# Mixing two tanh terms: one accumulator with av and minus av, in place of a difference on GpSimd

## The chip, the cores and the metric

The kernel runs on one core of one Trainium2 chip. A core has five engines that run side by side: TensorE (PE in the profile; its weight loads are listed as PEld), VectorE (DVE), ScalarE (ACT), GpSimd (POOL) and SyncE (SP), which here only issues DMA transfers. Each engine takes its own instructions in order; semaphores tie the engines to one another. The metric is the device time of one execution in microseconds (us). Lower is better.

## The reference

Four graph layers work on x of shape (8, 2048, 64): 8 batches, 2048 nodes, 64 features. Each layer takes a layer norm and a ReLU of x, computes its own output from that, and adds the output to x. The change lies at the end of the first layer. There every node has two vectors of 64 features: `industry`, a product with the adjacency matrix, and `g`, an attention over hyperedges. They are mixed with a softmax over two scores:

```
def attn_scores(f):
    return jnp.tanh(f @ fcW + fcb) @ av
pair = jnp.stack([industry, g], axis=2)
coefs2 = jax.nn.softmax(attn_scores(pair), axis=-1)
out = jnp.einsum('bnk,bnkf->bnf', coefs2, pair)
```

`fcW` maps 64 features to 128, and `av` has 128 entries. A softmax over two scores needs only their difference d: the weight of `industry` is (1 + tanh(d / 2)) / 2. The second layer begins with the norm of the mixed x, and then with the product of the adjacency matrix with it.

## The kernel before, in words

Features lie on the partitions and nodes along the free axis. Two batches share the 128 partitions (64 each), so there are four batch pairs q. The 2048 nodes are cut into four chunks of 512. `mix` (L619) goes over chunks and, within a chunk, over the four q: 16 pairs of chunk and q in all. The two inputs are `ind` (industry) and `g`, whole in SBUF.

`attend` (L644) does the first half of a pair. For `ind` and then for `g`, two matmuls with `fcw` fill a PSUM tile p1 of 128 x 2 x 512 (one half for each batch of the pair), and ScalarE writes its tanh into a slot of `ring` (L653); the ring has four slots, two for each of two pairs in flight. GpSimd subtracts the two tanh (L655) into dt, one of two buffers. At q = 0 the chunk's x is loaded by SP (L658), and GpSimd adds g to x for this q (L660). The loop in `mix` calls `attend` for the next pair before it finishes the present one: two matmuls multiply dt with `av`, copied into 64 equal columns, into the two 64-partition halves of a PSUM tile pd; ScalarE takes tanh of half of it (L684); VectorE forms ind - g (L686), scales it by the result (L687) and adds it to x (L688). So every partition of a batch holds the same score difference.

After the four pairs of a chunk, x is stored to DRAM (L241) and the norm for the next layer begins (`norm_parts`, L253): matmuls with `center` take off the mean, ScalarE squares (L264) and takes the ReLU (L269), matmuls with `to_rows` gather the means of the squares, ScalarE takes the root (L272, behind a load of its table), VectorE the reciprocal (L273). The generator then stops and is taken up after one of the next chunk's pairs: matmuls with `from_rows` spread the reciprocal back over the partitions, and VectorE writes the product (L634), two instructions for each q. The PSUM tiles of center, to_rows, from_rows and of the transposes come from one pool of three banks, `bank`.

`each` (L760), called ahead of a chunk's first pair, brings the rows of g for this chunk by four indirect DMAs on GpSimd (L763), transposes them on PE (L769), four transposes to a tile, and copies them into `g` by ScalarE and VectorE in turn (L172, L174).

The next layer (`chebyshev_layer`) begins with `by_node`, which turns the normed x into rows by transposes (L1312), split into a rounded high part by ScalarE (L232) and a rest by VectorE (L233). `adj_product` (L302) loads the adjacency in pieces (SP, L313) into three buffers, casts each on ScalarE (L325), and multiplies both parts on PE. All matmuls issued through the helper `mm` carry its line, L166, in the profile; they are told apart by the names of their tiles.

The order of the instructions on each engine isn't the order of the Python lines: the tile framework that the kernel is built with orders them, and an instruction whose buffers are free early can be placed ahead of other work. The order of the built program is therefore looked at beside the diff. The code has a second path for inputs that don't pass a check of their structure; it calls `mix` too, and does not run here.

Of the kernel before, what the change touches and what calls it, by code (L numbers as in the profile page):

```python
# [7 lines left out]
F = mybir.dt.float32  # L8
# [11 lines left out]
P = 128  # L20
NB = 8
N = 2048
D = 64
# [3 lines left out]
CW = 512  # L27
# [100 lines left out]
class Kernel:  # L128
# [490 lines left out]
    def mix(self, slots, ind, g, fcw, av, each=None):  # L619


        nc, tc = self.nc, self.tc
        big = [slots.tile([P, 2, NP, CW], F, name=f"mix{i}", tag=f"q{6 + i}") for i in range(3)]
        ring = slots.tile([P, 4, 2, CW], F, name="tanh", tag="q9")

        end = [slots.tile([P, 2, NP, CW], F, name=f"end{i}", tag=f"q{4 + i}") for i in range(2)]
        end = end[0][:, 0], end[0][:, 1], end[1][:, 0]
        xe, xo = self.chebyshev(slots)

        def write(q, ch, xr, scale):  # L630
            s = slice(ch * CW, (ch + 1) * CW)
            for i, dst in enumerate((xe, xo)):
                h = slice(i * D, (i + 1) * D)
                nc.vector.tensor_mul(dst(q)[h, s], xr[h], scale[h])  # L634


        with (
            tc.tile_pool(reuse_waits="tile", name="mix", bufs=2) as w,
            tc.tile_pool(reuse_waits="tile", name="mix_ps", bufs=1, space=PSUM) as ps,
        ):  # L640
            def bank():
                return ps.tile([P, CW], F, name="bank", bufs=3)

            def attend(ch, q):  # L644

                s = slice(ch * CW, (ch + 1) * CW)
                th = [ring[:, 2 * (q % 2) + i] for i in range(2)]
                for i, src in enumerate((ind, g)):
                    p1 = ps.tile([P, 2, CW], F, name="p1", bufs=2)
                    for half in range(2):  # L650
                        h = slice(half * D, (half + 1) * D)
                        self.mm(p1[:, half], fcw[h], src(q)[h, s])
                    nc.scalar.activation(th[i], p1, AF.Tanh, bias=self.col("fcb"))  # L653
                dt = w.tile([P, 2, CW], F, name="dt")
                nc.gpsimd.tensor_sub(dt, th[0], th[1])  # L655
                if q == 0:
                    bufs[ch] = end if ch == NC - 1 else [b[:, ch % 2] for b in big]
                    nc.sync.dma_start(bufs[ch][0], self.xs[0][ch])  # L658
                x = bufs[ch][0]
                nc.gpsimd.tensor_add(x[:, q], x[:, q], g(q)[:, s])  # L660
                return dt

            norm = iter(())
            bufs = {}
            if each is not None:
                each(0, bank)
            pairs = [(ch, q) for ch in range(NC) for q in range(NP)]
            ahead = attend(*pairs[0])
            for ch in range(NC):
                s = slice(ch * CW, (ch + 1) * CW)  # L670
                x, sq, xr = bufs[ch]
                for q in range(NP):
                    dt = ahead
                    if q == NP - 1 and each is not None and ch + 1 < NC:
                        each(ch + 1, bank)
                    if (ch, q) != pairs[-1]:

                        ahead = attend(*pairs[NP * ch + q + 1])
                    pd = ps.tile([P, CW], F, name="pd")
                    for half in range(2):  # L680
                        self.mm(pd[half * D : (half + 1) * D], av[:, :D], dt[:, half])

                    t2 = w.tile([P, CW], F, name="t2")
                    nc.scalar.activation(t2, pd, AF.Tanh, scale=0.5)  # L684
                    df = w.tile([P, CW], F, name="df")
                    nc.vector.tensor_sub(df, ind(q)[:, s], g(q)[:, s])  # L686
                    nc.vector.scalar_tensor_tensor(df, t2, 1.0, df, op0=OP.add, op1=OP.mult)  # L687
                    nc.vector.scalar_tensor_tensor(  # L688
                        x[:, q], df, 0.5, x[:, q], op0=OP.mult, op1=OP.add
                    )  # L690
                    if q < 2:
                        next(norm, None)
                self.store_x(0, ch, x)
                std = w.tile([P, CW], F, name="std")
                norm = self.norm_parts(ch, x, xr, sq, std, bank, write, nc.scalar)
            for _ in norm:
                pass
# [1666 lines left out]
```

## Time and profile before

| what | value |
|---|---|
| median of 3 runs | 2153.69 us (2149.0 to 2154.99) |
| profiled execution, its own time | 2148.51 us |
| its span, first to last instruction | 2146.8 us |
| mean granted TensorE clock | 0.932 |
| busy share PE / DVE / ACT / POOL | 89 / 53 / 33 / 33% |
| GpSimd differences (L655) | 16, 40.6 us busy |

The profile is one execution. It has a page with busy shares, 40 equal slices of the span, the chain of work that ended last and the costliest groups of instructions; the trace behind it also answers questions about a stretch: busy time of each engine, waits (who waited for whom), groups of instructions with their mean length, and the timeline. In a group, the numbers after the bar are its busy time in us, its mean length in ns, and the idle time of the engine just before it with what ended it. A float32 matmul of 512 columns shows as two records, so the two matmuls of a pd are four. The granted clock is the share of full speed at which TensorE was let run.

### The profile page before, as it was taken

To read this page: it belongs to the slowest core of one execution; us is meant where nothing else is said; L and a number is where in the kernel's file an instruction comes from. 1 tells how busy PE (TensorE), PEld (TensorE's weight loads), DVE (VectorE), ACT (ScalarE), POOL (GpSimd) and SP (SyncE) were. 2 spreads that over 40 slices of the span, in tenths; PEclk is the share of its full clock that TensorE was granted. 3 is DMA by queue.
4 is the path that set the end of the run, shared out by engine and by line. 5 is a ranking of instruction groups with operands and counts; after the bars stand their busy time and mean duration, and the time that the engine had idled before them with its cause. 6 is when DMAs were issued, how large, how long until landed. Compare 5 with 4: busy or idle time off the path is not lost. (4 is left out here: it accounts for less than half of the span.)

```text
span 2146.8 us, 21291 instructions
## 1 busy us (share of the span) xinstructions
PE 1914.5 (89%) x7461; PEld 1153.1 (54%) x7466; DVE 1134.1 (53%) x1932; ACT 714.7 (33%) x1351; POOL 702.4 (33%) x595
## 2 busy tenths in 40 slices
PE   5868999977779999999999998999999999679875
PEld 1425766642237774353443543677777666345432
DVE  7877677737660224424334255698603222249774
ACT  6412555535543440020100201335335333258400
POOL 0000466765300006617357065001000000177770
PEclk8868999988869999999999999999999999879997
DMA  8230333441034360140320401456533443475665
GB/s 320 82 110 4 102 104 118 133 171 43 36 94 134 119 177 14 32 125 0 102 56 5 118 1 60 138 186 235 166 118 125 151 145 131 158 210 162 180 181 180
DMA packets 108797, 253.66 MB, mean 118 GB/s; under 512 B 20912, under 2 KB 21056, under 8 KB 101376
## 3 DMA queue, kind: packets, MB, share of 16 engines
q1 hardware_dynamic: 89264, 181.45, 26.7%
q0 software_dynamic: 17104, 66.47, 10.0%
q10 hardware_dynamic: 2304, 4.20, 0.5%
q8 instruction: 63, 1.03, 0.2%
q14 instruction: 62, 0.51, 0.1%
HBM read 218.30 MB, written 33.78 MB: 117 GB/s over the span
## 5 line engine op out<-in xcount | busy, mean ns | idle before, releaser
L325 ACT CAST adj<-adj_t 128x512 fp32r<-128x512 f32 x384 | 237.3, 619 | 685.9 <-PE pp L166 349.5
L1421 POOL TENSOR_TENSOR acc<-acc,y 128x512 f32<-128x512 f32 x224 | 277.1, 1268 | 444.9 <-DVE y L1416 444.9
L166 PE MATMUL pp<-adj,hi 128*128 128x512 f32 x1280 | 364.4, 404 | 4.4 <-ACT adj L325 4.2
L166 PE MATMUL pk<-q,w 128*128 128x512 f32 (+1 forms) x1024 | 356.5, 609 | 1.8 <-ACT q L1389 1.6
L166 PE MATMUL pp<-adj,lo 128*128 128x512 f32 x1280 | 356.3, 398 | 0.0
L166 PEld LDWEIGHTS pp<-adj,hi 128*128 128x128 f32 x1280 | 241.2, 190 | 77.0 <-issue 16.2
L166 PEld LDWEIGHTS pp<-adj,lo 128*128 128x128 f32 x1280 | 242.7, 190 | 55.6
L166 PEld LDWEIGHTS pk<-q,w 128*128 128x128 f32 (+1 forms) x1024 | 136.2, 188 | 210.2 <-issue 165.9
L1416 DVE SCALAR_TENSOR_TENSOR y<-pk,bias,q 128x512 f32<-128x512 f32 x224 | 157.7, 745 | 142.7 <-PE pk L166 133.2
L166 PE MATMUL acc<-q,ident 128*128 128x512 f32 x416 | 203.4, 615 | 28.4 <-DVE q L2151 16.4
L2061 POOL DMA_INDIRECT ring<-f_rows,near x121 | 140.3, 1160 | 67.5 <-issue 30.2
L166 PEld LDWEIGHTS acc<-q,ident 128*128 128x128 f32 x416 | 76.7, 195 | 104.7 <-issue 47.7
L2165 POOL IOTA q<- 128x2048 int32 x1 | 1.8, 1834 | 316.6 <-PE p L166 316.6
L166 PE MATMUL pp<-adj,x_ind_hi 128*128 128x512 f32 x256 | 94.7, 487 | 2.1 <-DVE q L751 1.9
L166 PE MATMUL bank<-std,from_rows 32*128 32x512 f32 x128 | 45.5, 858 | 54.4 <-DVE std L273 34.5
L1853 POOL TENSOR_TENSOR q<-q,beta 128x512 f32<-128x512 f32 x57 | 67.9, 1192 | 54.6 <-DVE beta L1829 30.8
L1416 DVE SCALAR_TENSOR_TENSOR acc<-pk,bias,q 128x512 f32<-128x512 f32 x32 | 22.6, 746 | 118.1 <-PE pk L166 118.1
L2132 DVE TENSOR_TENSOR q<-ring,e 128x1024 f32<-128x1024 f32 x58 | 70.0, 1218 | 9.3 <-PE acc L166 9.1
L273 DVE RECIPROCAL std<-std 128x512 f32<-128x512 f32 x16 | 53.6, 3351 | 36.7 <-ACT std L272 36.6
L166 PE MATMUL pp<-adj,x_ind_lo 128*128 128x512 f32 x256 | 71.7, 399 | 0.0
L1543 POOL DMA_INDIRECT q<-in_adj_dram,order x15 | 17.2, 1146 | 160.3 <-DVE top L1557 134.0
L166 PEld LDWEIGHTS pp<-adj,x_ind_hi 128*128 128x128 f32 x256 | 48.5, 190 | 38.7 <-issue 23.7
(410 smaller groups left out, 2695.8 us busy)
## 6 DMA issues: line engine op xcount, KB each, us to landing
adj_t<-in_adjT_dram SPq DMA_DIRECT2D x128, 512.0 KB, 3.9
adj_t<-in_adjT_dram SPq DMA_DIRECT2D x128, 256.0 KB, 3.3
rows<-in_adj_dram SPq DMA_DIRECT2D x16, 1024.0 KB, 6.0
q<-x SPq DMA_DIRECT2D x10, 1024.0 KB, 4.8
x<-q SPq DMA_DIRECT2D x9, 1024.0 KB, 4.0
q<-in_embT_dram SPq DMA_DIRECT2D x8, 1024.0 KB, 12.1
x_ch<-in_xT_dram SPq DMA_DIRECT2D x4, 1024.0 KB, 6.0
h_rows<-q SPq DMA_DIRECT2D x16, 256.0 KB, 3.6
```

The costliest lines, as they stand in the source:

```text
L166: self.nc.tensor.matmul(out, lhsT, rhs, start=start, stop=stop)
L273: nc.vector.reciprocal(std, std)
L325: nc.scalar.copy(moving, at[:, i])
L1416: nc.vector.scalar_tensor_tensor(y, pks[b, half], bias[:, b : b + 1], emb[:, b], op0=OP.add, op1=OP.mult,)
L1421: nc.gpsimd.tensor_add(acc, acc, y)
L1543: nc.gpsimd.indirect_dma_start(row, None, self.a["adj"], bass.IndirectOffsetOnAxis(ap=order[:, 1, t : t + 1], axis=0),)
L1853: self.nc.gpsimd.tensor_tensor(x, x, by.unsqueeze(2).to_broadcast([P, NB, D]), op=OP.mult)
L2061: self.nc.gpsimd.indirect_dma_start(to, None, self.kern.f_rows[:], bass.IndirectOffsetOnAxis(ap=index, axis=0))
L2132: nc.vector.tensor_tensor(y.rearrange("n i (b f) -> n i b f", b=NB), block[:, i : i + 2, : NB * D].rearrange("n i (b f) -> n i b f", b=NB) ...
L2165: nc.gpsimd.iota(whole, pattern=[[1, N]], base=0, channel_multiplier=0)
```

## The change

The tanh of both inputs go to the second product as they are. Per pair there are four matmuls instead of two: av times the first tanh opens the accumulation in each half of pd, and minus av (`less`, made once by VectorE) times the second tanh closes it. The difference on GpSimd and its two buffers are gone.

```diff
@@ -651,15 +651,16 @@
                         h = slice(half * D, (half + 1) * D)
                         self.mm(p1[:, half], fcw[h], src(q)[h, s])
                     nc.scalar.activation(th[i], p1, AF.Tanh, bias=self.col("fcb"))
-                dt = w.tile([P, 2, CW], F, name="dt")
-                nc.gpsimd.tensor_sub(dt, th[0], th[1])
                 if q == 0:
                     bufs[ch] = end if ch == NC - 1 else [b[:, ch % 2] for b in big]
                     nc.sync.dma_start(bufs[ch][0], self.xs[0][ch])
                 x = bufs[ch][0]
                 nc.gpsimd.tensor_add(x[:, q], x[:, q], g(q)[:, s])
-                return dt
-
+                return th
+
+            less = w.tile([P, D], F, name="less", bufs=1)
+            nc.vector.tensor_scalar_mul(less, av[:, :D], -1.0)
+            avs = av[:, :D], less
             norm = iter(())
             bufs = {}
             if each is not None:
@@ -670,15 +671,19 @@
                 s = slice(ch * CW, (ch + 1) * CW)
                 x, sq, xr = bufs[ch]
                 for q in range(NP):
-                    dt = ahead
+                    th = ahead
                     if q == NP - 1 and each is not None and ch + 1 < NC:
                         each(ch + 1, bank)
                     if (ch, q) != pairs[-1]:
 
                         ahead = attend(*pairs[NP * ch + q + 1])
                     pd = ps.tile([P, CW], F, name="pd")
-                    for half in range(2):
-                        self.mm(pd[half * D : (half + 1) * D], av[:, :D], dt[:, half])
+                    for i in range(2):
+                        for half in range(2):
+                            self.mm(
+                                pd[half * D : (half + 1) * D], avs[i], th[i][:, half],
+                                start=i == 0, stop=i == 1,
+                            )
 
                     t2 = w.tile([P, CW], F, name="t2")
                     nc.scalar.activation(t2, pd, AF.Tanh, scale=0.5)
```

In the built program two more things differ, both on engines that the diff doesn't name. The first four adjacency loads of the second layer (L313) stand on SP's queue directly behind the load of the last chunk's x, and three of their casts (L325) stand on ScalarE among the first pairs of the mixing; before, these loads followed the mixing's last store. And the first 16 matmuls of the second layer's adjacency product are placed between the transposes L1312, from the fifth group of four on; before, they followed them.

## The prediction

> **What bounds the kernel now.** I first read the page's slices. TensorE (PE) is busy in nine tenths of nearly every slice; the soft place is around slices 9 to 12, where its granted clock is 0.7 to 0.9. The chain that ended last covers only the last 17 us of the span, so it says nothing here. The edited code runs from 462 to 606 us ("the mixing stage"), which I split where the gather transposes of each 512-node chunk begin. Columns: stretch, its length, busy time of PE, of weight loads, of VectorE, ScalarE, GpSimd, then granted clock, DMA share, GB/s.
>
> ```profile
> 487.40:524.30 36.90, 28.53 (x91) 9.19 (x89) 28.09 (x27) 19.61 (x27) 16.16 (x9) 0.85 0.16 57
> 524.30:564.07 39.77, 30.76 (x91) 10.67 (x89) 25.65 (x25) 19.60 (x27) 16.04 (x9) 0.80 0.06 27
> 564.07:601.87 37.80, 28.47 (x91) 9.34 (x89) 26.34 (x25) 19.52 (x27) 15.96 (x9) 0.86 0.07 28
> ```
>
> Three periods, 114.5 us; no engine is full, so a chain of waits bounds them, with PE the fullest. PE idles 26.7 us of it. A mean clock near 0.84 means, if it only alternates between half and full, about 31% of the time at half. Next the waits and groups of 465 to 612 us:
>
> ```profile
> PE pd L166 <- POOL dt L655: 17.3, 5, 5.6
> PE bank L166 <- DVE q L634: 12.1, 3, 4.0
> L655 POOL TENSOR_TENSOR dt<-tanh 128x1024 f32<-128x1024 f32 x16 | 40.6, 2543 | 61.5 <-ACT tanh L653 61.4
> L686 DVE TENSOR_TENSOR df<-q,q 128x512 f32<-128x512 f32 x16 | 26.9, 1684 | 0.4
> L687 DVE SCALAR_TENSOR_TENSOR df<-t,df 128x512 f32<-128x512 f32 x16 | 26.0, 1624 | 25.0 <-ACT t L684 25.0
> L166 PE MATMUL pd<-dt,av 128*64 128x512 f32 x64 | 22.0, 773 | 17.3 <-POOL dt L655 17.3
> ```
>
> PE, which takes its work in order, stands 17.3 us in five waits for GpSimd's difference. L686 and L687 average 1.6 us, while their shortest is 0.68. Last the timeline, for the period from 564.07 and the step after the stage (start, length, engine, line, idle before):
>
> ```profile
> 570.52 1.99 PE L166 MATMUL p<-q,fcw 64*128 64x512 f32 x8
> ...
> 573.96 5.54 POOL L655 TENSOR_TENSOR dt<-tanh 128x1024 f32<-128x1024 f32 x2
> ...
> 576.79 1.08 PE L166 MATMUL pd<-dt,av 128*64 128x512 f32 x4 [4.29 <-POOL dt L655]
> ...
> 577.80 5.39 PE L166 MATMUL bank<-mix,center 128*128 128x512 f32 x8
> ...
> 591.29 2.52 DVE L687 SCALAR_TENSOR_TENSOR df<-t,df 128x512 f32<-128x512 f32 x1 [0.96 <-ACT t L684]
> ...
> 596.05 2.04 PE L166 MATMUL bank<-std,from_rows 32*128 32x512 f32 x2 [4.04 <-DVE q L634]
> ...
> 600.03 1.90 PE L166 MATMUL pd<-dt,av 128*64 128x512 f32 x4
> ...
> 623.07 10.38 PE L1312 MATMUL pt<-ident,q 64*128 64x64 f32 x100 [1.77 <-DVE lo L233]
> ...
> 637.59 2.08 PE L166 MATMUL pp<-adj,hi 128*128 128x512 f32 x4
> ```
>
> Both tanh of the pair were ready by 570.9, but GpSimd did its four adds of the chunk (568.16 to 574.0) first; the difference came at 576.8. PE sat 4.29 us, and the centers behind ran partly at half speed (0.86 us instead of 0.43 per output). At 591.29 the next difference stretched L687 to 2.52 us, which held the first L634, which frees the PSUM bank of the fourth from_rows: a second idle of 4.04 us, again followed by half speed (pd 1.90 against 1.08).
>
> **What the skill says.** "TensorE: Matmul & The Clock Gate", What's actually happening: the array clock falls to half after about one idle window of 3.4 us, and returns after about as much sustained work. The trace agrees: after the 2.20 us idle at 500.7 pd took 1.08; after 4.29 and 5.65 us it, or the centers behind it, ran at half. "GPSIMD Engine Reference", Specifications: GpSimd shares its SBUF interfaces with VectorE and contends with VectorE instructions with two SBUF inputs. L686 and L687 have two; 1.6 us against 0.68 agrees. "TensorEngine Tiling (Array Packing)", Column Tiling and Key Properties: 64-wide stationaries run as two column tiles, and changing the tiling mode drains TensorE. The two 64-row halves of pd indeed start together (two records at 500.73, two at 501.21).
>
> **The change, part by part.** *Removed:* 16 GpSimd subtractions, 40.6 us of GpSimd, so five PE waits (17.3 us) and their share of the VectorE stretching. GpSimd keeps its 16 adds, which still stretch some L686 to L688.
>
> *Added:* per pair of chunk and batch pair, four more matmul records on PE. No row accumulates onto an av product; the nearest is p, where four further records lengthen 1.13 us to 1.99: 0.86 us, or 1.62 at half clock (1.98 to 3.60 at 479). Sixteen make 13.8 us at full clock, 16.4 at clock 0.84, 26 at half. The other bound is 3.2 each at half clock, should the two halves not overlap. I take 0.86. The tanh buffers are now freed by pd, which stands on PE ahead of the p whose tanh reuses them: no new wait. The one negation on VectorE is 128x64 (a 128x1024 one, L1294, takes 0.68 us) and falls while PE waits for gathers near 457: nothing.
>
> *Moved*, by the order of the built program: without dt's two buffers, the first four loads of layer 1's adjacency (512 KB each) go on SP's queue behind the last chunk's input load (465.76 us), ahead of the chunk 0 store, and three casts (L325, 0.62 us) go on ScalarE ahead of the first t2 and the third pair's tanh. The input load takes 7.1 us to land (472.9); 512 KB at the burst's 410 GB/s is 1.3 us, so the casts can begin at 474 to 476. The fourth load waits for the second cast; behind it on SP is a store not ready before 500. In layer 1's first step, 16 adjacency matmuls are put between the transposes L1312. GpSimd's last four gathers now follow one another; used only from 560.
>
> *First chunk.* pd of pair 0 no longer waits for gathers and adds (5.65 us idle): it runs at 471.4 to 473.3, p(2) to 475.2, pd(1) to 477.1; tanh(2) behind the casts starts at 477.6, p(3) runs 478.7 to 480.6, pd(2) ends at 482.5 where the transposes began at 487.4. **-5** (-2 to -6).
>
> *One period*, walked from 564.07 at full clock (the 16 pairs are numbered 0 to 15; this is chunk 3, pairs 12 to 15): transposes and p of the first pair, with their wait for the bank, to 568.9; pd(11), now 1.87 long, to 570.8; p(13) to 572.7; pd(12) directly to 574.6; centers (4 x 0.86) to 578.1; to_rows and p(14) to 582.5; pd(13) to 584.4. ScalarE: squares until 579.6, table load 1.28, root at 581.6. VectorE: reciprocal 3.35, to 585.0. PE: three from_rows to 586.3. L687 is 0.69 now and L688 0.69, so L634's first two end at 588.6 (PE idle 2.3 us, under the window, clock stays); fourth from_rows and p(15) to 590.5; pd(14) to 592.4, where it ended at 601.9. That is -9.5, three times -28.5.
>
> The same by terms: 17.3 of waits, three times 1.83 of stretched L687 (5.5), half-clock excess about 13.7 in the periods (27 busy us at half, halved) and 2.5 in the first chunk, against 13.8 added: -25. Between -33.5 (walk, first chunk included) and -25 I take **-29**; neither counts all hops between engines.
>
> *Layer 1's first step.* Transposes and the first 16 adjacency matmuls now take 620.12 to 643.71, 23.6 us, at clock 0.5 until 642. Where the program already mixes them (670.5 to 672.6, full clock), one transpose group plus one matmul takes 0.70 against 0.23 and 0.20 apart: a switch costs about 0.27. At full clock 16 x 0.70 + 16 x 0.20 = 14.4, so VectorE's 16.5 bounds: -7. At half clock, 28: +5. I take **-2**.
>
> After that the order is as before, PE is busy 99% of 640 to 720 us, and a shift passes to the end. Sum: -29 - 2 = -31. The profiled execution took 2148.51 (span 2146.8), the median is 2153.69; 2148.5 - 31 = 2117.5, and against the median **2123**.
>
> **Rivals.** *B, the clock doesn't recover*: 17.3 + 5.5 back, 16.4 added, nothing in layer 1: -6, **2147**. For it: the clock is 0.84 even where PE is busy 75%; against: each half-speed stretch I looked at follows an idle of 4 us or the low-density transposes. *C, the interleaving of layer 1 fails* at half clock: -29 + 5 = -24, **2130**. For it: clock 0.50 all through 620 to 640. *D, slower*: the two halves of the second product don't overlap, or drain, and the clock stays low: 16 x 3.2 = 51 against 22.8, +28, **2182**; it decides once a pair's addition exceeds 22.8 / 16 = 1.4 us without clock recovery. Against: pd's four records already overlap. *That the change doesn't do what it says* can't be: no subtraction is left on GpSimd.
>
> **Numbers.** Main case 0.68 (own range 2104 to 2136), C 0.10, B 0.15, D 0.07. About 0.3% (6.5 us) is what a measurement tells from no change; B lies on that edge, so half of it counts as same. Faster 0.85, same 0.08, slower 0.07. Range 2103 to 2145: left out are D, half of B and a sliver of the main case.
>
> **What would show it.** No L655 row; pd about 1.9 us per group of eight records; PE waiting under 5 us for tanh at pd; periods near 29 us with clock above 0.95; L687 near 0.7 us; mixing ending some 29 us earlier; matmuls of L166 among L1312's. Wrong if the periods stay over 35 us, if pd's eight records take 3 us or more at full clock, or if ScalarE's casts wait past 480.

## The result, and the profile after

| | before | after |
|---|---|---|
| median, runs beside one another | 2152.06 us (2149.0 to 2154.99) | 2132.72 us (2121.22 to 2136.89) |
| ratio, with its 95% interval | | 0.9906 (0.9881 to 0.9931) |
| profiled execution, its span | 2148.51, 2146.8 us | 2136.79, 2134.9 us |
| mean granted clock of the span | 0.932 | 0.932 |

The changed kernel is 19 us faster where 31 were forecast; 2132.72 us is 10 us above the forecast median.

To find where the difference lies, both spans are cut at the same events of the trace: the first transpose of gathered rows, the first transpose of the second layer (`pt`), and the first matmul into the tile `pk`, which follows that layer's first adjacency product.

| stage (us) | before | after | difference |
|---|---|---|---|
| up to the first gather transpose | 455.9 | 458.0 | +2.1 |
| mixing | 164.2 | 140.3 | -23.9 |
| second layer, first step | 186.6 | 190.0 | +3.4 |
| all that follows | 1340.1 | 1346.6 | +6.5 |
| span | 2146.8 | 2134.9 | -11.9 |

The line numbers shift a little: L684, L686 and L687 are now L689, L691 and L692, and L1312 is L1317. L166, L325, L634 and L653 are the same. In the experiments they shift by a few lines again; the operation and the tiles in a line tell what it is. First the mixing by chunks, cut as in the prediction (stretch, length, busy time of PE, weight loads, VectorE, ScalarE, GpSimd, then granted clock, DMA share, GB/s):

```profile
484.79:515.90 31.11, 29.00 (x106) 9.70 (x104) 20.07 (x25) 19.53 (x27) 5.85 (x4) 0.95 0.18 68
515.90:547.02 31.12, 29.01 (x107) 9.80 (x105) 20.16 (x25) 19.52 (x27) 5.85 (x4) 0.95 0.08 34
547.02:579.45 32.43, 30.32 (x106) 9.90 (x104) 20.15 (x25) 19.52 (x27) 6.06 (x5) 0.90 0.08 33
```

The periods fell from 36.9, 39.8 and 37.8 us to 31.1, 31.1 and 32.4, and PE idles about 2.1 us in each, where it idled 26.7 us in the three together. The clock rose from 0.80 to 0.86 to between 0.90 and 0.95, so it isn't full. The waits and the groups of 465 to 605 us:

```profile
PE bank L166 <- DVE q L634: 7.9, 4, 2.1
```

```profile
L166 PE MATMUL pd<-tanh,av 128*64 128x512 f32 x64 | 19.8, 700 | 1.6 <-ACT t L689 1.6
L691 DVE TENSOR_TENSOR df<-q,q 128x512 f32<-128x512 f32 x16 | 18.7, 1172 | 0.4
L166 PE MATMUL pd<-tanh,less 128*64 128x512 f32 x64 | 17.6, 630 | 0.0
...
L692 DVE SCALAR_TENSOR_TENSOR df<-t,df 128x512 f32<-128x512 f32 x16 | 11.3, 703 | 24.4 <-ACT t L689 24.4
```

The five waits for GpSimd are gone, and the scaling of the difference (L692) is back at 0.70 us from 1.62. The subtraction of the inputs (L691) still averages 1.17 us: twelve of its sixteen instances take 0.68 or 0.69 us, and the four that run beside the adds that GpSimd kept take 1.51 to 5.91. What is left on PE within the periods is one wait for VectorE's L634 in each, 2.1 us at most. The timeline of the chunk from 547.02 shows what that wait does (start, length, engine, line, idle before):

```profile
555.81 1.08 PE L166 MATMUL pd<-tanh,av 128*64 128x512 f32 x4
...
556.72 1.03 PE L166 MATMUL pd<-tanh,less 128*64 128x512 f32 x4
...
557.68 3.70 PE L166 MATMUL bank<-mix,center 128*128 128x512 f32 x8
...
572.54 1.37 PE L166 MATMUL bank<-std,from_rows 32*128 32x512 f32 x2 [2.11 <-DVE q L634]
...
575.84 1.97 PE L166 MATMUL pd<-tanh,av 128*64 128x512 f32 x4
...
577.60 1.92 PE L166 MATMUL pd<-tanh,less 128*64 128x512 f32 x4
```

The second product costs what was estimated: eight records of pd from 555.81 to 557.68, 1.87 us, and the eight centers behind them run at full speed. But the fourth from_rows waits 2.11 us, and what follows it runs at half speed: 1.97 and 1.92 us for four records of pd that take 1.08 and 1.03 at full clock.

In the second layer's first step, transposes and adjacency matmuls now alternate:

```profile
601.96 0.79 PE L166 MATMUL pp<-adj,hi 128*128 128x512 f32 x1
...
602.69 0.70 PE L1317 MATMUL pt<-ident,q 64*128 64x64 f32 x8
```

All 32 groups of transposes and the first 32 adjacency matmuls took 27.3 us before (620.12 to 647.38) and take 29.9 us now (598.32 to 628.25). The mean clock over the first 40 us of this step is 0.72 before and 0.67 after; the half speed in which the step begins lasts 22.6 us before and 26.1 us after.

### The profile page after: what moved, and what is told of

Its sections match the earlier page's. It is cut to its first block, busy times and chain, and to the rows that moved or that the text cites. A ratio compares the mean times of both kernels' runs of the same rounds, so it can differ in the third digit from the quotient of the medians.

```text
span 2134.9 us, 21390 instructions
## 1 busy us (share of the span) xinstructions
PE 1929.4 (90%) x7525; PEld 1154.3 (54%) x7530; DVE 1111.8 (52%) x1933; ACT 714.7 (33%) x1351; POOL 666.9 (31%) x579
## 3 DMA queue, kind: packets, MB, share of 16 engines
q0 software_dynamic: 17104, 66.47, 10.2%
q8 instruction: 63, 1.03, 0.2%
## 5 line engine op out<-in xcount | busy, mean ns | idle before, releaser
L325 ACT CAST adj<-adj_t 128x512 fp32r<-128x512 f32 x384 | 237.3, 619 | 689.4 <-PE pp L166 345.8
L166 PE MATMUL pp<-adj,hi 128*128 128x512 f32 x1280 | 368.8, 406 | 4.9 <-ACT adj L325 3.7
L166 PE MATMUL pk<-q,w 128*128 128x512 f32 (+1 forms) x1024 | 358.3, 611 | 3.8 <-ACT q L1394 3.6
L166 PE MATMUL pp<-adj,lo 128*128 128x512 f32 x1280 | 361.1, 400 | 0.0
L166 PEld LDWEIGHTS pp<-adj,hi 128*128 128x128 f32 x1280 | 241.7, 191 | 78.4 <-issue 16.7
L166 PEld LDWEIGHTS pp<-adj,lo 128*128 128x128 f32 x1280 | 243.0, 190 | 56.4
L166 PEld LDWEIGHTS pk<-q,w 128*128 128x128 f32 (+1 forms) x1024 | 136.6, 188 | 213.5 <-issue 166.4
L166 PE MATMUL acc<-q,ident 128*128 128x512 f32 x416 | 202.7, 613 | 28.2 <-DVE q L2156 17.9
L166 PEld LDWEIGHTS acc<-q,ident 128*128 128x128 f32 x416 | 76.1, 193 | 103.8 <-issue 46.6
L166 PE MATMUL pp<-adj,x_ind_hi 128*128 128x512 f32 x256 | 94.6, 486 | 2.2 <-DVE q L756 1.9
L166 PE MATMUL bank<-std,from_rows 32*128 32x512 f32 x128 | 43.7, 858 | 48.6 <-DVE std L273 34.5
L1421 DVE SCALAR_TENSOR_TENSOR acc<-pk,bias,q 128x512 f32<-128x512 f32 x32 | 22.6, 746 | 121.5 <-PE pk L166 121.5
L166 PE MATMUL pp<-adj,x_ind_lo 128*128 128x512 f32 x256 | 71.6, 398 | 0.0
L166 PEld LDWEIGHTS pp<-adj,x_ind_hi 128*128 128x128 f32 x256 | 48.5, 189 | 38.8 <-issue 23.8
L1548 POOL DMA_INDIRECT q<-in_adj_dram,order x15 | 17.2, 1148 | 166.3 <-DVE top L1562 137.5
## 6 DMA issues: line engine op xcount, KB each, us to landing
q<-in_embT_dram SPq DMA_DIRECT2D x8, 1024.0 KB, 12.6
```

Of the source, the lines that this page charges most:

```text
L166: self.nc.tensor.matmul(out, lhsT, rhs, start=start, stop=stop)
L325: nc.scalar.copy(moving, at[:, i])
L1421: nc.vector.scalar_tensor_tensor(y, pks[b, half], bias[:, b : b + 1], emb[:, b], op0=OP.add, op1=OP.mult,)
L1548: nc.gpsimd.indirect_dma_start(row, None, self.a["adj"], bass.IndirectOffsetOnAxis(ap=order[:, 1, t : t + 1], axis=0),)
```

## The experiments

Every trace was cut into the stages above; the table collects their lengths, in us. "Kept" means that the second layer's loads, casts and first adjacency matmuls stand where they stood before the change, "moved" that they stand where the change put them. The medians come from several series; each run was timed beside the kernel before, and its ratio below refers to that.

| run | order of layer 2 | mixing | first step | what follows | median |
|---|---|---|---|---|---|
| before | kept | 164.2 | 186.6 | 1340.1 | 2152.06 |
| after | moved | 140.3 | 190.0 | 1346.6 | 2132.72 |
| e1, the changed kernel again | moved | 140.8 | 189.8 | 1333.8 | 2130.53 |
| e2, changed, order kept | kept | 138.4 | 189.2 | 1335.2 | 2123.51 |
| e3, before, order moved | moved | 164.8 | 189.7 | 1339.8 | 2156.02 |
| e4, changed, idle subtraction | kept | 152.3 | 188.3 | 1343.3 | 2142.55 |
| e5, e2 with a later from_rows | kept | 130.7 | 186.8 | 1338.1 | 2113.22 |
| e6, e2 with one product | kept | 129.8 | 187.3 | 1346.6 | 2121.22 |
| e7, before with two products | kept | 170.1 | 185.1 | 1344.6 | 2158.11 |
| e8, difference on VectorE | kept | 147.1 | 187.1 | 1338.7 | 2134.1 |
| e9, e5 with one product | kept | 123.9 | 186.8 | 1344.8 | 2112.41 |
| e10, e8 with the later from_rows | kept | 143.3 | 188.0 | 1340.3 | 2128.8 |
| e11, e5 with the order moved | moved | 132.2 | 191.2 | 1336.0 | 2127.27 |

### e1: the changed kernel again

No edit.

> The changed kernel once more. Theory (waits, stretched VectorE and clock returned in the mixing stage): the stage from the first gather transpose to the first L1312/L1317 transpose again takes 140 us (138 to 143) where it took 164, in the profile. The profiled run of the changed kernel gave back some 11 us after layer 1's start (788 us on), most of it where the granted clock was lower. If that is only where the clock's windows happen to fall, the median lies between 2121 and 2133 and single runs differ by 10 us and more, and the later stretches of this profile differ from the first one's by several us. Rival, the change itself slows the later layers: the same stretches lose the same 3 to 5 us each again, and the median is 2133 to 2138.

2130.53 us (2123.25 to 2131.47), ratio 0.9904 (0.9884 to 0.9925). Mixing and first step repeat within 0.5 us; "what follows" is 12.8 us shorter than in the first profile. So the 6.5 us lost there in the first profile are not a steady effect of the change. No line of that code is edited, and over all the kernels this part takes between 1333.8 and 1346.6 us. Single spans can therefore not be compared closer than that. The mixing can; the first step, over the nine profiles with the order kept, varies by 4 us (185.1 to 189.2).

### e2: the move of the second layer's loads undone

An unused tile takes the place of the freed buffers:

```diff
+            room = w.tile([P, 2, CW], F, name="room")
+            nc.gpsimd.memset(room[:, 0, :1], 0.0)
```

> The changed kernel with two unused buffers of dt's size kept, so that the adjacency loads, casts and matmuls of layer 1 stand where they stood before the change. Theory: the mixed order of layer 1's first step costs 2 to 4 us, so this runs 1 to 4 us faster than the changed kernel, and from the first transpose to the 32nd adjacency matmul it takes 27 us where the changed kernel took 29.9. Rival, the early loads and casts are a part of the gain: 3 us or more slower than the changed kernel.

2123.51 us (2119.99 to 2134.38), ratio 0.9886 (0.9862 to 0.9911). The median is 7 us below the changed kernel, where 1 to 4 were expected; the mixing and the first step explain 2.7 of them. The mixing is 1.9 us shorter, of which only 0.3 lie in the first chunk, where the three casts stood; 1.6 lie in the last, whose clock is 0.91 instead of 0.86. The first step did not return to 186.6 us in this profile. Its first 40 us did (PE busy 36.13 us at clock 0.73, before 36.14 at 0.72). Later, where transposes and adjacency matmuls alternate, the granted clock is 0.50 from 646.4 to 653.2 us, which costs 3.4 us:

```profile
642.98:646.39 3.41, 3.26 (x19) 1.94 (x19) 3.25 (x6) 1.90 (x4) 0.00 (x0) 1.00 0.46 150
646.39:653.22 6.83, 6.83 (x29) 4.63 (x30) 0.85 (x2) 1.95 (x5) 0.00 (x0) 0.50 0.26 79
```

PE was busy for 3.26 of the 3.41 us before it, so this fall of the clock did not follow an idle gap. What set it off is not known.

### e3: the move alone

The kernel before, with the difference written over the first tanh, so that its two buffers are free and the order moves as in the changed kernel:

```diff
-                dt = w.tile([P, 2, CW], F, name="dt")
+                dt = th[0]
                 nc.gpsimd.tensor_sub(dt, th[0], th[1])
```

> The kernel before, with the difference written over the first tanh: the subtraction on GpSimd and its wait stay, dt's buffers go, and with them layer 1's loads, casts and matmuls move as in the changed kernel. Theory: the mixing stage stays near 164 us, layer 1's first step is 2 to 4 us longer, in all 2151 to 2158. Rival, the move is what gained: 2130 to 2140.

2156.02 us (2147.68 to 2162.85), ratio 1.0027 (1.0015 to 1.004). The first 40 us of the first step (stretch, length, busy times of the five columns, clock, DMA share, GB/s), for this run and then for the kernel before:

```profile
622.18:662.18 40.00, 38.84 (x206) 26.11 (x206) 17.54 (x40) 16.23 (x41) 0.00 (x0) 0.68 0.29 80
```

```profile
620.12:660.12 40.00, 36.14 (x217) 30.32 (x217) 16.71 (x40) 18.51 (x45) 0.00 (x0) 0.72 0.40 116
```

PE is busier by 2.7 us and gets through 206 records instead of 217. The first step is 3.1 us longer than before, and the mixing, with periods of 36.5 and 38.2 us, gains nothing. The median is 6 us higher, as expected. So the move is not what gained.

### e4: the subtraction kept, its result unread

The changed kernel, and GpSimd still forms the difference, into buffers that no instruction reads:

```diff
+                dt = w.tile([P, 2, CW], F, name="dt")
+                nc.gpsimd.tensor_sub(dt, th[0], th[1])
```

> The changed kernel with the GpSimd subtraction put back into a dt that nobody reads (order of layer 1 as before the change): no wait of TensorE for it, but the work beside VectorE's. Theory, three terms: only the stretch of VectorE comes back, L692 (L687 before) at 1.4 to 1.6 us where it is 0.70, 1.8 us in each of three periods and some clock with it, so 4 to 10 us slower than the changed kernel with the two unused buffers, periods of 33 to 35 us. Rival, contention was most of the loss: periods of 36 to 38 us and 2145 or more. Rival, contention cost nothing: within 2 us.

2142.55 us (2131.96 to 2153.98), ratio 0.9956 (0.994 to 0.9972). The median is 19 us above e2, where 4 to 10 were expected, and the mixing takes 14 us more, although nothing reads the result. The groups and the waits of 465 to 605 us show two ways by which it reaches PE:

```profile
L694 DVE SCALAR_TENSOR_TENSOR df<-t,df 128x512 f32<-128x512 f32 x16 | 26.9, 1682 | 26.7 <-ACT t L691 26.7
```

```profile
PE bank L166 <- DVE q L634: 11.8, 3, 3.9
...
ACT tanh L653 <- POOL dt L655: 6.4, 2, 4.0
```

L694, the scaling, is back at 1.68 us and so delays L634 and the fourth from_rows, by 3.9 us at most as before the change; and ScalarE waits for the ring slots that the subtraction still reads. The second was not in the forecast. Of the 25.8 us by which the mixing of e2 is shorter than before, 14 are lost again when the instruction merely runs, so more than half of the saving needed it gone, and not only its result unneeded. How the 14 us divide between the two ways is not shown.

### e5: a later fourth from_rows

The walk of the prediction rested on the clock staying full through the wait at the fourth from_rows. This run, e2 with one more edit, fills that wait: the generator of the norm stops once more, ahead of its last from_rows, and goes on one pair later.

```diff
+            if relus is not None and q == NP - 1:
+                yield
...
-                    if q < 2:
+                    if q < 3:
                         next(norm, None)
```

> The changed kernel with the two unused buffers (order of layer 1 as before), and the norm's last from_rows and its two products taken one pair later: between the third from_rows, which leaves no free bank, and the fourth now stand a p and a pd whose inputs are ready. Theory: the prediction's walk failed at this place; TensorE's idle of 2.1 us before the fourth from_rows was taken as too short for the clock to fall, and the clock fell for one window of 3.4 us in each period. With the idle filled, periods take 28 to 29.5 us instead of 31.1, and the median is 5 to 9 us under the same kernel without this move. Rival, the periods are bound by TensorE's work and the half-speed windows belong to something else: periods stay at 30.5 to 31.2 us, the time within 2 us.

2113.22 us (2108.59 to 2126.8), ratio 0.9834 (0.9807 to 0.9862): 10 us below e2, where 5 to 9 were expected, and the fastest version that computes the whole result. The mixing is 7.7 us shorter. Its two middle periods, and the timeline where the wait stood:

```profile
480.59:507.90 27.31, 27.31 (x106) 9.42 (x104) 17.13 (x21) 20.12 (x28) 5.87 (x4) 1.00 0.20 77
507.90:537.65 29.75, 27.71 (x106) 9.11 (x105) 20.06 (x26) 19.65 (x27) 5.92 (x4) 1.00 0.09 36
```

```profile
512.29 1.07 PE L778 MATMUL bank<-ident,q 128*128 128x128 f32 x8 [1.67 <-issue]
...
532.60 1.13 PE L166 MATMUL bank<-std,from_rows 32*128 32x512 f32 x6
533.67 1.13 PE L166 MATMUL p<-q,fcw 64*128 64x512 f32 x4
534.73 1.08 PE L166 MATMUL pd<-tanh,av 128*64 128x512 f32 x4
535.64 1.03 PE L166 MATMUL pd<-tanh,less 128*64 128x512 f32 x4
536.60 1.12 PE L166 MATMUL bank<-std,from_rows 32*128 32x512 f32 x2
```

Work that stood behind the wait now fills it, the clock is 1.00, and PE in the first of these periods is busy without a gap. The periods are 27.3 and 29.8 us, on both sides of the walk's 28.3. Another idle of 1.67 us, ahead of the gather transposes, did not lower the clock.

### e6: one product instead of two

e2 without the second product; the score of g is left out of the computation.

```diff
-                    for i in range(2):
-                        for half in range(2):
-                            self.mm(
-                                pd[half * D : (half + 1) * D], avs[i], th[i][:, half],
-                                start=i == 0, stop=i == 1,
-                            )
+                    for half in range(2):
+                        self.mm(pd[half * D : (half + 1) * D], av[:, :D], th[0][:, half])
```

> The changed kernel with the two unused buffers, without the second product: pd is av times the tanh of industry alone, so the score of g is left out. Theory: a pair's second product takes 0.95 us of TensorE and little of it hides, so the mixing stage is 11 to 16 us shorter (122 to 127 us where it was 138.3). Rival, the added matmuls were hidden in waits: under 5 us.

2121.22 us (2118.69 to 2123.14), ratio 0.9862 (0.9841 to 0.9884). The mixing falls by 8.5 us to 129.8, where 11 to 16 were expected; the medians of e2 and e6 lie too close to be told apart. A period of it, and its timeline:

```profile
509.19:538.74 29.55, 26.65 (x91) 8.99 (x89) 20.72 (x25) 19.30 (x27) 5.84 (x4) 0.90 0.09 36
```

```profile
533.40 1.49 PE L166 MATMUL bank<-std,from_rows 32*128 32x512 f32 x2 [2.22 <-DVE q L634]
...
536.83 1.97 PE L166 MATMUL pd<-tanh,av 128*64 128x512 f32 x4
```

The wait of 2.2 us and the half speed behind it are still there: they belong to the norm, not to the second product. PE is busy 10.2 us less in the mixing (110.3 against 120.5 in e2), and 8.5 of them came back.

### e7: the second product in the kernel before

Before, with the product done twice with half of `av`; the difference stays on GpSimd.

```diff
-                    for half in range(2):
-                        self.mm(pd[half * D : (half + 1) * D], av[:, :D], dt[:, half])
+                    for i in range(2):
+                        for half in range(2):
+                            self.mm(
+                                pd[half * D : (half + 1) * D], less, dt[:, half],
+                                start=i == 0, stop=i == 1,
+                            )
```

> The kernel before with its product done twice with half of av each, same sum: the added matmuls alone, with GpSimd's difference and its wait in place. Theory: they stand behind the wait and ahead of the rest, so nothing hides them: 12 to 18 us slower than before, 2162 to 2168. Rival, they keep the clock up or fall into idle time: within 6 us.

2158.11 us (2153.08 to 2163.87), ratio 1.003 (1.001 to 1.0051). The group of pd, 455 to 615 us, with its idle time still 17.3 us for GpSimd:

```profile
L166 PE MATMUL pd<-dt,less 128*64 128x512 f32 x128 | 39.0, 739 | 17.4 <-POOL dt L655 17.3
```

pd's busy time rose by 17.0 us (39.0 against 22.0), PE's in the whole stage only by 10.0 (129.25 against 119.26), in part since at a mean clock of 0.85 against 0.82 other matmuls were shorter (p 46.9 us in all against 48.7, centers 12.7 against 14.8), and its idle time fell by 4.2 (40.8 against 45.0). So the stage grew by 5.9 us. The expected 12 to 18 did not come: the median is 7 us above the kernel before. Here added PE work paid for part of itself.

### e8: the difference on VectorE

```diff
-                nc.gpsimd.tensor_sub(dt, th[0], th[1])
+                nc.vector.tensor_sub(dt, th[0], th[1])
```

> The kernel before with the difference on VectorE in place of GpSimd, no added matmuls. A 128x1024 difference takes about 1.2 us there, 19 us in all. Theory (it was the wait behind GpSimd's adds and the slow GpSimd that cost, not the difference itself): mixing stage 132 to 145 us, 2115 to 2130 in all, near the changed kernel. Rival, VectorE's queue becomes the bound: the stage stays over 150 us.

2134.1 us (2132.02 to 2140.64), ratio 0.9932 (0.9913 to 0.995); the mixing takes 147.1 us, 17.1 less than before. That is two thirds of the 25.8 us that e2, with the same order of the second layer, gains in this stage; they come without a second product, by taking the difference off GpSimd. The timeline of the chunk from 517.62 shows why it is not as good:

```profile
522.03 6.29 POOL L660 TENSOR_TENSOR mix<-mix,q 128x512 f32<-128x512 f32 x4 [27.20 <-ACT q L172]
...
523.77 1.75 DVE L686 TENSOR_TENSOR df<-q,q 128x512 f32<-128x512 f32 x1
...
528.79 2.35 DVE L655 TENSOR_TENSOR dt<-tanh 128x1024 f32<-128x1024 f32 x2
...
530.06 1.98 PE L166 MATMUL pd<-dt,av 128*64 128x512 f32 x4 [3.45 <-DVE dt L655]
...
531.96 4.52 PE L166 MATMUL bank<-mix,center 128*128 128x512 f32 x6
```

A difference takes 1.2 us, but VectorE's L686 ahead of it takes 1.75 us beside GpSimd's adds (0.68 at its shortest). The difference comes late, PE waits 3.45 us, and pd and a part of the centers run at half speed. Not tried was a difference left on GpSimd but placed ahead of its adds.

### e9: one product, and the later from_rows

Both edits of e5 and of e6; the score of g is left out again.

> The version with the late fourth from_rows, with only the product of the first tanh (the score of g is left out, as in the run without the second product). Theory: what ate the saving of that run were the idle time of about 2.1 us before the fourth from_rows and the half-clock windows behind it; with the idle filled, PE is the bound and the 13.8 us of the second product come back nearly in full: mixing 118 to 123 us against 130.7 with both products, periods 24 to 26 us with a clock of 0.98 or more, time 2099 to 2107. Rival: ScalarE and VectorE stand right behind PE, so the periods stay at 27 us or more with idle time on PE in other places, mixing 126 to 131, time 2108 to 2114.

2112.41 us (2107.4 to 2113.89), ratio 0.9808 (0.9788 to 0.9828). The mixing takes 123.9 us, 6.9 less than e5: between the two expectations. Its middle periods:

```profile
479.00:504.19 25.19, 24.07 (x90) 8.31 (x89) 17.52 (x22) 19.94 (x29) 5.85 (x4) 1.00 0.26 94
504.19:532.22 28.03, 24.43 (x88) 7.97 (x89) 20.65 (x26) 19.29 (x27) 5.84 (x4) 1.00 0.09 38
```

At clock 1.00 the second product is 3.2 us of PE per period (27.31 less 24.07), 0.81 us per pair. Of it 1.7 to 2.1 us come back; the rest turns into idle time, ahead of tanh and of the gather transposes. So at full clock the second product costs some 2 us per chunk. Over the whole mixing it costs 6.9 us here, 8.5 in e6 and 5.9 in e7, always less than the 13.8 of PE work. In the time of the whole kernel e9 and e5 can't be told apart: this run's last part took 6.7 us more than that of e5, with no edit there. Why, stays open.

### e10: the VectorE difference, with the later from_rows

The edits of e5 and of e8.

> The kernel before with the difference on VectorE and, in addition, the late fourth from_rows. Theory: the late from_rows removes the waits of 6.5 us for L634 and their half-clock windows, but not the 10.3 us in which PE waits for the difference while GpSimd's adds stretch VectorE: mixing 137 to 141 us against 147.1, time 2122 to 2128, so 9 us or more above the same with two products. Rival: the VectorE difference then costs no more than the second product, mixing 129 to 133, time 2112 to 2116.

2128.8 us (2127.39 to 2133.98), ratio 0.9896 (0.9874 to 0.9918). PE's waits of 455 to 600 us:

```profile
PE pd L166 <- DVE dt L657: 12.2, 5, 3.1
...
PE bank L166 <- DVE q L636: 2.8, 3, 1.6
```

The mixing fell by 3.8 us, where 6 to 10 were expected. The waits for the fourth from_rows fell from 6.5 to 2.8 us and the mean clock rose from 0.83 to 0.86, but PE idles 35.1 us in this stage against 34.5 in e8: new waits, ahead of the gather transposes above all, took the place of those removed. The wait for the difference, 13.2 us in e8, stays at 12.2. To e5 12.6 us remain in the mixing and 15.6 in the medians. So in this pair of kernels two products beat a difference on VectorE.

### e11: the later from_rows in the changed kernel as it is

e5 without the unused tile, so the order of the second layer moves.

> The changed kernel with the late fourth from_rows but without the unused buffers, so the second layer's loads, casts and first 16 adjacency matmuls stand where the change put them. Theory: the move costs what it cost elsewhere, about 2.5 us in the mixing and 1 to 3 us in the second layer's first step: mixing 132 to 134, first step 189 to 191, time 2116 to 2120 against 2113. Rival: it costs nothing measurable, 2111 to 2115.

2127.27 us (2117.84 to 2133.67), ratio 0.9895 (0.9867 to 0.9922). The mixing is 1.5 us longer than in e5, all of it in the first chunk (26.2 against 24.7), where the casts stand, and the first step is 4.4 us longer. With the changed kernel, e1 and e3 that makes four profiles with the order moved, whose first step takes 189.7 to 191.2 us, on average 190.2; the nine with the order kept take 185.1 to 189.2, on average 187.2. The half speed at the start of the step lasts 25.8 to 27.8 us where the order is moved and 20.1 to 23.1 where it is kept. So the move costs some 3 us in this step. The median is 7 us above the expected range and 14 above e5, of which these two stages explain 5.9; the profiled run, at 2117.84, was the fastest of the four. The rest is open.

## Why the prediction was right, and where it was not

The direction and most of the mechanism held. Of the 31 us forecast, -23.9 (mixing) and +3.4 (first step), together -20.5, are found in the two stages that the change touches, close to the 19 us between the medians. The other two stages of the profile (+2.1 and +6.5) have no edit, and the last of them varies by as much when the same kernel runs again.

**Waits and stretching removed: right.** No PE wait for GpSimd's difference is left (17.3 us before), and L687 fell from 1.62 to 0.70 us. The skill's page "GPSIMD Engine Reference" (Specifications) says that GpSimd contends with VectorE instructions with two SBUF inputs; e4 agrees (1.68 us with the unread subtraction, 0.70 without). The 14 us that it cost there also contain a wait for the ring.

**Second product, 0.86 us per pair: right as time on PE, too much as a cost.** The eight records take 1.87 us at full clock as walked, and the halves overlap, so D did not come. e9 gives 0.81 us. But of the 13.8 us that stand in the sum, 5.9 to 8.5 showed in the length of the mixing (e6, e7, e9).

**First chunk, -5: right.** 31.50 us became 26.75. ScalarE's last cast began at 478.99 us, before the 480 that would have been a sign against it.

**The period, -9.5 each: the failing step.** The periods gained 5.8, 8.7 and 5.4 us, 19.9 instead of 28.5. The step that failed is "PE idle 2.3 us, under the window, clock stays", a term of the walk put at nothing. The idle came out as foretold, 2.11 us, but the clock did not stay: the records behind it ran at half speed, and clocks of 0.95, 0.95 and 0.90 are worth 1.6, 1.6 and 3.2 us of the periods (one minus the clock, times the length), 6.4 in all. Some 2 us are left over the three periods; at the fourth from_rows the timeline was about a microsecond behind the walk, which had not counted every hop between engines. e5 shows that this wait is what lowered the clock: with it filled the clock is 1.00 and the periods are 27.3 and 29.8 us, on average near the walk's 28.3; e9 and e11, with the same edit, also have 1.00 in these periods.

The prediction used the skill's window of 3.4 us (page "TensorE: Matmul & The Clock Gate", What's actually happening) as a threshold for one idle gap. It isn't one here: 2.11 us lowered the clock in this kernel and 2.22 us in e6, while 2.20 us at 500.7 had not in the kernel before. Nor is 2.1 us the threshold. Gaps of 1.67 us did not lower it in e5, but gaps of 1.62 us in e10 and 1.63 in e8 were followed by half speed, and so was one of 1.45 us in the kernel before. That one could have been read ahead of the forecast:

```profile
491.39 0.66 PE L769 MATMUL bank<-ident,q 128*128 128x128 f32 x4 [1.45 <-DVE q L174]
491.98 3.29 PE L166 MATMUL p<-q,fcw 64*128 64x512 f32 x6
```

```profile
489.09:492.50 3.41, 1.96 (x7) 0.73 (x7) 3.41 (x6) 0.58 (x2) 0.76 (x1) 1.00 0.00 0
492.50:495.92 3.42, 3.42 (x8) 1.12 (x8) 1.85 (x3) 1.66 (x2) 3.38 (x3) 0.50 0.00 0
```

Six records of p take 1.98 us at full clock; here 3.29. In all thirteen traces the granted clock is either 1.00 or 0.50 and changes only on a grid of 3.41 us, which lies differently in each run. So the place of a gap in that grid may matter: the 2.20 us at 500.7 are cut by it into 0.80 and 1.40, and the next piece is at full clock, while the 2.11 us before 572.54 lie in one piece. It isn't all: in e2 a gap of 2.11 us was cut into 1.03 and 1.09, and half speed still followed. What decides is open; between 1.45 and 2.20 us the length of the gap alone does not.

**The sum by terms, -25: near the -23.9 measured, in part by luck.** In the three periods its terms let PE's idle time fall by 17.2 us (17.3 without the first chunk's 5.65, and 5.5) and its busy time by 3.4 (13.7 of half speed less 10.3 of added work). Idle time fell by 20.4 us and busy time rose by 0.6: two misses of 3 to 4 us that cancel. Choosing -29, nearer the walk, was the worse choice, since both counts assumed a full recovery of the clock and the walk no hops.

**Layer 1's first step, -2: wrong in sign.** It cost 3.4 us, and 3.1 in e3, without the second product. This is rival C's mechanism: the alternation ran at half clock, one pair of a transpose group and an adjacency matmul each 1.35 us. C's bound of +5 was nearer than the value taken. That C's 2130 also lies near the time measured is partly luck, since C took the mixing at -29.

**After that the order is as before: right** as to the work; but the part behind varies by 13 us from profile to profile, which no step had allowed for.

**Rival B** failed as a whole, since the mean clock in the periods rose by 0.04 to 0.15, but its doubt was justified: the clock did not come back in full.

## What to carry to other kernels

Before paying for an engine's result by more matmuls, ask what that engine does to the others while it runs: here an unread GpSimd subtraction cost 14 us, more than half of what the mixing had gained. Then look for the next wait behind the one removed and put ready work of the same engine ahead of it: the one extra stop of a generator took 7.7 us more off the mixing. An idle gap on PE can cost its length and the half speed behind it, so look in the trace for what followed gaps of that size, short ones too. And look at what freed buffers let the framework move.

## What the runs showed of the hardware

- Single idle gaps on PE were followed by half speed at 1.45 us (before), 1.62 (e10), 1.63 (e8) and 2.11 (after), and were not at 1.67 (e5, e9, e11) and 2.20 (before). The granted clock is 1.00 or 0.50, in pieces of 3.41 us.
- The clock also fell where PE was busy for 3.26 of 3.41 us, in an alternation of 64 x 64 transposes and adjacency matmuls (e2, 646.4 us).
- With a GpSimd subtraction of 128 x 1024 float32 running in each pair, VectorE's scaling of 128 x 512 took 1.68 us on average, without it 0.70 (e4 against e2). In e4 it took 0.68 us where no GpSimd arithmetic ran beside it (489.34 us) and 2.52 where the subtraction did for 1.97 us of it (512.03).
- Added matmuls of 17.0 us in a stage with clock 0.82 lengthened it by 5.9 us (e7); the second product taken out of a stage with clock 0.89 shortened it by 8.5 us (e6), of one with 0.93 by 6.9 (e9).
- Transposes of 64 x 64 in alternation with adjacency matmuls had a lower mean clock over 40 us (0.65 to 0.68 in four profiles) than transposes first and matmuls after (0.71 to 0.75 in nine).
